# Output products ahead of the small convolution matmuls in pairs with in_proj alone, VectorE copies, later stores and later last scans

## The chip, the cores and the metric

The kernel runs on one core of a Trainium2 chip. The metric is the device time of one execution in microseconds (us), the median of several executions. A core has TensorE (PE) for matrix products, VectorE (DVE), ScalarE (ACT), GpSimd (POOL), and SyncE (SP), whose queue issues the DMA transfers here. TensorE writes its products to PSUM, 8 banks of 512 fp32 columns on 128 partitions. All data are fp32.

## The reference

For 4 images of 128 channels on 96x96 pixels, the reference normalises in groups of 4 channels (`_gn`), lays the pixels out in four orders (rows, rows reversed, columns, columns reversed), runs one sequence model on each, and fuses the four results.

```
def _scan1d(x, ...):
    t = _grouped1x1(x, in_proj_w, in_proj_b, G)
    u, gate = (t[:, :HID], t[:, HID:])
    u = jax.nn.silu(u)
    u = lax.conv_general_dilated(u, dw_w, ..., feature_group_count=HID)
    s = _conv1x1(u, ssm_in_w)
    a = DMIN + (DMAX - DMIN) * jax.nn.sigmoid(_conv1x1(u, ssm_delta_w, ssm_delta_b))
    a = jnp.clip(a, 0.0001, 0.9999)
    bb = jnp.tanh(_conv1x1(u, ssm_b_w, ssm_b_b))
    cc = jnp.tanh(_conv1x1(u, ssm_c_w, ssm_c_b))
    prefix = jnp.cumsum(jnp.log(a), axis=-1)
    hst = jnp.exp(prefix) * jnp.cumsum(bb * s * jnp.exp(-prefix), axis=-1)
    u = u + _conv1x1(cc * hst + ssm_d[None, :, None] * s, ssm_out_w)
    u = _grouped1x1(u * jax.nn.sigmoid(gate), mix_w, mix_b, G)
    return _conv1x1(u, out_proj_w, out_proj_b)
...
x = x + _L0_conv_ref(_gn(x), ...)
```

Here HID is 256 channels, the convolution has 5 taps, and the recurrent state has 32 channels. The log/exp/cumsum lines are the recurrence h = a*h + b*s.

## The kernel before, in words

**Tiling.** An image is done in two phases, one for the two column orders ("V") and one for the two row orders ("H"): 8 phases. In a phase two streams s = 0, 1 run together, which are one order and its reverse. A phase has 6 steps of 4 pairs. A pair (the function `pair(t)`, t from 0 to 191) takes one of 4 interleaved quarters of a step for both streams, 384 columns each. So a phase is 24 pairs, and t modulo 24 tells what a pair contains.

**Stages of a pair on TensorE**, with letters that the text uses:

- F, in_proj (`compute_front`), for the pair four ahead. The four results stand in banks 7, 6 (stream 0) and 2, 3 (stream 1), and ScalarE turns them into `sil` with a silu (L471). It is done only for the first 3 steps of a phase. The other 3 steps read the same columns backwards, with the streams exchanged. Steps 2 and 3 of a phase share a tile; the silus of steps 0 and 1 of a phase are stored to DRAM (L447, `kept_sil`) and loaded again.
- C, the convolution of the first 128 channels of u by `band` matrices (`conv`), and L, its remaining part with the small `less` matrices (`conv_less`), into one bank for each stream. ScalarE copies both banks to `us[i][:, s, 0, :]` (L589). The other 128 channels are convolved by VectorE, four `taps` at L606 after a first one on ScalarE (L604).
- W, the output product with `w_fin` (`accumulate`), for the pair seven back: a bank for each of two streams; ScalarE copies each to `ys` (L707, L709), and GpSimd adds it to `acc` in SBUF (L723).
- O, the state's product (`out_of`, L488), for the pair six back, into banks 0 to 3, which ScalarE has filled with u beforehand (`under`, L496) in many pairs. VectorE multiplies with the gates (`gating`, L558).
- G, the gates (`gate`, L482), in those pairs that make gates. ScalarE takes their tanh (L504).
- P, the projections (`proj`), always into banks 4 and 5. The first half of P reads the channels that VectorE convolved, the second those copied at L589. Then ScalarE (L634 to L636) and GpSimd make the recurrence's coefficients. VectorE runs the recurrence of a whole step in two scans (L676) in the first two pairs of the next step, and clips some coefficients (L764) in the last two. GpSimd makes the input of O from it (`outputs`, L682 to L684).

**Kinds of pairs**, by t modulo 24. 0 to 5 and 20 to 23: in_proj but no gates (the gates are old ones, loaded from DRAM); this is `with_front` and `old` in the code. 6 and 7: in_proj and gates. 8 to 17: gates alone. 18 and 19: neither. The first six pairs of the kernel have no `back` part (no W, O or gating). The last four pairs (188 to 191) have no in_proj.

**Banks.** `plan` gives C and W their banks. In a pair with in_proj, C and L use banks 4 and 5 and W uses 7 and 6. In the others it is the reverse.

**Order.** Each engine runs its instructions in the order in which the functions issue them; from `pair(0)` on the code is under a manual schedule. Before that (the first in_proj, statistics, weights) the framework orders them. In a pair with in_proj alone the TensorE order is F, C, L, W, O, P. In pairs with gates alone, and in those with neither, it is C, W, L, then G and O, or O alone, then P. The lines that decide it are L766 to L794 of `pair`. Between the stages of ScalarE in such a pair with in_proj alone stand, in this order: four silus, two copies of u, two `under`, two copies to `ys`.

After the 192 pairs, `tail()` finishes the last six units: it clips, runs the last step's two scans on VectorE, and then for each of six pairs O, gating, `under` of the next, W.

In the third and fourth pair of each step of a V phase of the first three images VectorE also takes statistics of the next image (`stats_chunks`, L397), and small pieces of `stats_finish` follow in the H phase.

Of the kernel before, what the change touches and what calls it, by code (L numbers as in the profile page):

```python
# [66 lines left out]
def conv_preact_kernel(  # L67
# [56 lines left out]
    def plan(with_front):  # L124

        return (PROJ, FRONT[:2]) if with_front else (FRONT[:2], PROJ)

    def bank(i):
        return psum[:, i, :]
# [119 lines left out]
    def load_front(step, s, r, q):  # L249
        if fresh(step):  # L250
            un = units[step * UB + s]
            nc.sync.dma_start(
                x_in[s][r, q, :], xs[un["b"], un["lay"], r, q, bass.ds(un["st"] * N, N + 1)]
            )
# [155 lines left out]
        for e in range(2)  # L410
    ]

    def front(i, banks, streams=range(2)):
        for _ in front_parts(i, banks, streams):
            pass

    def front_parts(i, banks, streams=range(2)):

        step, g = divmod(i, R)
        if step * UB >= NU:  # L420
            return
        st = step % NS
        if st == NS // 2:
            sils[step] = sils[step - 1]
            load_silu(step + 1, (g,))
        elif st == NS - 1 and g < 2:
            load_silu(step, (2 * g, 2 * g + 1))
        elif g == 0 and fresh(step):
            sils[step] = wk.tile([P, 2, 2, 4, N + 1], F32, tag="sil", name=f"sil_{step}")
        if fresh(step):  # L430
            yield from compute_front(step, g, banks, streams)
        sil = sils[step]

        if st == 0:
            engine = nc.gpsimd if step else nc.vector
            for s in range(2):
                engine.memset(sil[64 * s : 64 * s + 64, s, 0, g, 0:1], 0.0)
            if g < 2:
                engine.memset(sil[:, :, 1, g, 0:1], 0.0)

        for s in range(2):
            load_front(step + 1, s, slice(64 * s + 32, 64 * s + 64), slice(g, g + 1))
        if g == R - 1:
            for s in range(2):
                load_front(step + 1, s, slice(64 * s, 64 * s + 32), slice(0, R))
        if st < NS // 2 - 1:
            nc.sync.dma_start(kept_sil[step // NS % 2][st][g], sil[:, :, :, g, :])  # L447

    def load_silu(step, gs):
        if 0 in gs:  # L450
# [3 lines left out]
                sils[step][:, :, :, g, :], kept_sil[step // NS % 2][NS - 1 - step % NS][g]  # L454
            )

    def compute_front(step, g, banks, streams):
        un = units[step * UB]
        wn, bn = stats[un["b"]]
        sil = sils[step]  # L460
        for s in range(2):
            for j in range(2):
                r = slice(64 * s + 32 * j, 64 * s + 32 * j + 32)
                for c in range(4):
                    m, q = (c, g) if j else (g, R - 1 - c if s else c)
                    mm(bank(banks[2 * s + j]), c, wn[r, s, 32 * m : 32 * m + 32],
                       x_in[s][r, q, :], True, True)
        yield
        for s in streams:
            for j in range(2):  # L470
                nc.scalar.activation(  # L471
                    sil[:, s, j, g, :],
                    bank(banks[2 * s + j])[:, : N + 1],
                    AF.Silu,
                    bias=bn[:, 1:2] if j else bn[:, 4 + g : 5 + g],
                )
# [16 lines left out]
    def under(bi, s):  # L493

        seeded.add(bi)
        nc.scalar.copy(psum[:, SSM + 2 * s : SSM + 2 * s + 2, :N], us[bi][:, s])  # L496
# [80 lines left out]
                mm(bank(banks[s]), g, band[:, s, p, g, :], columns(step, sil[s][:, g, :], 1 - k),  # L577
                   True, False)

    def conv_less(i, banks):  # L580
        step, p = units[i]["step"], units[i]["p"]
        sil, k = blocks(step), less_of(p)
        for g in range(4):
            for s in range(2):
                r = less_rows(s, p)
                mm(bank(banks[s]), g, less[r, p, g, :], columns(step, sil[s][r, g, :], k),
                   False, True)
        for s in range(2):
            nc.scalar.copy(us[i][:, s, 0, :], bank(banks[s])[:, :N])  # L589

    def new_u(i):
        us[i] = wk.tile([P, 2, 2, N], F32, tag="u", bufs=LAG + 2, name=f"u_{units[i]['id']}")
# [149 lines left out]
    def pair(t):  # L742
        i, k, bi = 2 * t, t % R, 2 * (t - LAG)
        back = bi >= 0
        old = back and mirror(bi // 2) is not None

        late = bi > 2 and (bi - 2) % (NU // B) == 0
        with_front = fresh((t + R) // R)
        seed = old or back and not with_front
        banks, w = plan(with_front or not back)  # L750
        if back:
            front(t + R, FRONT, (1, 0) if old else (0, 1))
        if seed and not with_front:
            under(bi, 1)
        send()

        if len(reload) == 4 and (k == 1 or late):
            for b, r in reload:
                nc.sync.dma_start(accf[:, r], xr[b, :, r])
            reload.clear()  # L760
        new_u(i)
        taps(i, range(1, K))
        if t and clip_late(i - 2):
            nc.vector.tensor_scalar(*decay(i - 2)[1])  # L764
        conv(i, banks)
        if with_front or not back:  # L766
            conv_less(i, banks)
        if not back:
            first_tap(i + 2)
            front(t + R, FRONT)  # L770
        recurrence(t)
        un = units[i]
        stats_chunks(t)

        def stats_piece():
            if later and k > 1:
                next(later[0], None)

        if with_front or not back:
            free[0] = w[1]  # L780
            stats_piece()
        if seed and with_front:
            for s in (1, 0):
                under(bi, s)
        if waiting and not late:
            accumulate(waiting.pop(0), w[0])()
        if seed and not with_front:
            under(bi, 0)
        if old or not with_front:
            accumulate(waiting.pop(0), w[1])()  # L790
        if back and not with_front:
            free[0] = w[0]
            stats_piece()
            conv_less(i, banks)  # L794
        if old:
            for s in range(2):
                for j in range(2):
                    out_of(bi, s, j)
                load_gate(bi + s + UB)
        elif back:  # L800
            gates_and_out(bi, with_front)
        if back:
            for s in range(2):
                gating(bi, s)
        if un["order"] == "V" and un["b"] + 1 < B and un["st"] == NS - 1 and k == R - 1:
            later[:] = [stats_finish(un["b"] + 1)]
        if t + 1 < NU // 2:
            load_chunks(t + 1)
        if back:
            load_kept(bi // 2 + 2)  # L810
            if waiting:
                add = accumulate(waiting.pop(0), w[1])
                if not late:
                    add()
            first_tap(i + 2)
            scale_s(i - 2)
        if t == NU // 2 - 1:
            for s in range(2):
                under(bi + 2, s)
        proj(i, PROJ)  # L820
        if not back and t > 0:
            scale_s(i - 2)
        if late:
            add()
            accumulate(waiting.pop(0), w[1])()
        if back:
            waiting.extend(units[bi : bi + 2])
        if t == NU // 2 - 3:
            load_last()

        if bi > 0 and bi % (NU // B) == 0:
            send()

    def tail():

        first, banks = NU // 2 - LAG, (6, 7, 4, 5)

        for op in decay(NU - 2):
            nc.vector.tensor_scalar(*op)
        for part in range(2):  # L840
            scan(NU // UB - 1, part)
        scale_s(NU - 2)
        outputs(2 * first + 2)
        last = None
        for n in range(first, NU // 2):
            i = 2 * n
            for s in range(2):
                for j in range(2):
                    out_of(i, s, j)
            for s in range(2):  # L850
                gating(i, s)
                if i + 2 < NU:
                    under(i + 2, s)

            if last:
                last()
            if i + 4 < NU:
                outputs(i + 4, lambda *_: None)
            accumulate(waiting.pop(0), banks[2])()
            last = accumulate(waiting.pop(0), banks[3], nc.vector)  # L860
            if i + 4 < NU:
                nc.scalar.copy(tbs[i + 4][64:P, :], tbs[i + 4][0:64, :])
            send()
            waiting.extend(units[i : i + 2])
        last()
        for s in range(2):
            accumulate(waiting.pop(0), banks[2 + s], nc.vector, True)()
            send()
# [98 lines left out]
```

## Time and profile before

| what | us |
|---|---|
| five executions, median | 1872.89 |
| lowest and highest of them | 1872.38, 1874.05 |
| the profiled execution | 1873.79 |
| its span, first to last instruction | 1872.1 |
| ScalarE busy | 1544.7 |
| VectorE busy | 1553.5 |
| GpSimd busy | 1565.9 |
| pairs with in_proj alone, from one P to the next | 9.40 (the first of each four 9.46) |
| pairs with gates alone | 9.30 |
| pairs with neither | 8.25 |

The mean granted TensorE clock of the execution was 0.988. Read the span as stages, a pair of some 9 us each, since every stage has its own limit: the idle time of an engine in one pair says nothing of another. A timeline row names the start, the duration from the first start to the last end, the engine, the line, the operation, the tile written and those read, the shape, the number of instructions merged, and in brackets how long the engine had been idle before and what ended that. TensorE's rows overlap, since products are pipelined, so a stage's cost is the difference between its start and the next one's start. An fp32 product is two instructions in the counts.

### The profile page before, as it was taken

The numbers are of one execution on the slowest core, as the hardware profiler recorded it, in microseconds if no ns is written. First come the engines' busy times: TensorE is split into PE (matmuls) and PEld (weight loads), VectorE is DVE, ScalarE is ACT, GpSimd is POOL, SyncE is SP. The second block draws the span as 40 slices with busy tenths as digits, with TensorE's granted clock in tenths as the row PEclk, the third lists the DMA queues.
The fourth block names the chain that finished last, engine by engine and source line by source line (L and its number), as shares of the span: only waits on it lengthen the run. The fifth ranks groups of instructions, "written<-read, shape, count | busy, mean of one in ns | idle before, by whom it ended". The sixth has DMA issues, their size and how long they took to land. (4 is left out here: it accounts for less than half of the span.)

```text
span 1872.1 us, 57687 instructions
## 1 busy us (share of the span) xinstructions
PE 1833.6 (98%) x24024; PEld 691.7 (37%) x24024; DVE 1553.5 (83%) x1541; ACT 1544.7 (83%) x2873; POOL 1565.9 (84%) x1615
## 2 busy tenths in 40 slices
PE   5999999999999999999999999999999999999997
PEld 3234333443334433344333433344333443334432
DVE  4689888887888988888789898888887888788885
ACT  4788888888888888888888888888888888888875
POOL 5488988888879898888887989888888889988886
PEclk6999999999999999999999999999999999999998
DMA  7454473543875466243695556443476633635333
GB/s 241 118 192 155 140 220 100 174 151 127 274 249 189 155 183 208 84 158 121 207 298 190 170 167 202 143 139 117 156 232 217 231 136 125 205 100 171 145 130 142
DMA packets 147827, 321.20 MB, mean 172 GB/s; under 512 B 14192, under 2 KB 115696, under 8 KB 147568
## 3 DMA queue, kind: packets, MB, share of 16 engines
q1 hardware_dynamic: 147136, 316.56, 52.1%
q8 instruction: 190, 3.11, 0.7%
q10 hardware_dynamic: 432, 0.96, 0.1%
q14 instruction: 69, 0.57, 0.1%
HBM read 185.21 MB, written 132.25 MB: 170 GB/s over the span
## 5 line engine op out<-in xcount | busy, mean ns | idle before, releaser
L606 DVE SCALAR_TENSOR_TENSOR psum<-sil,small,psum 128x768 f32<-128x768 f32 x576 | 589.0, 1023 | 39.9 <-ACT psum L604 13.8
L133 PE MATMUL psum<-u,w_fin 128*32 128x384 f32 x6144 | 538.3, 489 | 0.3
L133 PE MATMUL psum<-u,main 128*32 128x384 f32 x6144 | 536.6, 490 | 0.7 <-DVE u L606 0.7
L558 DVE SCALAR_TENSOR_TENSOR u<-gate,psum 128x768 f32<-128x768 f32 x376 | 349.9, 953 | 199.4 <-ACT gate L504 86.8
L723 POOL TENSOR_TENSOR acc<-ys,acc 128x384 f32<-128x384 f32 x376 | 412.6, 1117 | 28.7 <-ACT ys L707 8.4
L682 POOL TENSOR_TENSOR t<-t,t 64x384 f32<-64x384 f32 x192 | 262.1, 1365 | 79.7 <-DVE t L676 66.5
L496 ACT COPY psum<-u 128x768 f32<-128x768 f32 x352 | 279.0, 810 | 40.2 <-DVE u L606 28.6
L133 PEld LDWEIGHTS psum<-u,w_fin 128*32 128x32 f32 x6144 | 189.0, 110 | 318.5 <-issue 219.4
L133 PEld LDWEIGHTS psum<-u,main 128*32 128x32 f32 x6144 | 182.3, 110 | 327.0 <-issue 247.3
L133 PE MATMUL psum<-sil,band 128*32 128x384 f32 x3072 | 289.0, 490 | 4.6 <-ACT tm L634 2.1
L683 POOL TENSOR_TENSOR t<-t,t 64x384 f32<-64x384 f32 x192 | 280.7, 1462 | 15.0
L639 POOL TENSOR_SCALAR t<-tm 64x384 f32<-64x384 f32 x191 | 177.6, 930 | 130.9 <-ACT tm L634 95.4
L604 ACT ACTIVATE psum<-sil,small 128x768 f32<-128x768 f32 x192 | 174.1, 907 | 125.9 <-DVE u L558 119.3
L488 PE MATMUL psum<-t,main 32*128 32x384 f32 x1536 | 239.4, 521 | 7.0 <-ACT psum L496 6.9
L642 POOL TENSOR_TENSOR t<-t,tm 64x384 f32<-64x384 f32 x192 | 208.9, 1088 | 15.3
L606 DVE SCALAR_TENSOR_TENSOR u<-sil,small,psum 128x768 f32<-128x768 f32 x192 | 194.9, 1015 | 7.8
L471 ACT ACTIVATE sil<-psum,bnorm 128x385 f32<-128x385 f32 x384 | 191.9, 584 | 10.8 <-PE psum L133 5.0
L504 ACT ACTIVATE gate<-psum,bnorm 128x384 f32<-128x384 f32 x384 | 193.4, 583 | 3.4 <-PE psum L488 1.8
L482 PE MATMUL psum<-x_in,wn 32*128 32x384 f32 x768 | 191.7, 521 | 0.4 <-ACT u L589 0.4
L709 ACT COPY ys<-psum 128x384 f32<-128x384 f32 x287 | 137.4, 479 | 53.3 <-PE psum L133 42.6
L589 ACT COPY u<-psum 128x384 f32<-128x384 f32 x384 | 165.4, 483 | 18.9 <-PE psum L133 13.1
L133 PE MATMUL psum<-sil,less 64*32 64x384 f32 x3072 | 168.4, 495 | 0.0
(86 smaller groups left out, 1637.1 us busy)
## 6 DMA issues: line engine op xcount, KB each, us to landing
sil<-sil SPq DMA_DIRECT2D x128, 770.0 KB, 6.2
kept<-gate SPq DMA_DIRECT2D x80, 768.0 KB, 3.9
gate<-kept SPq DMA_DIRECT2D x76, 768.0 KB, 4.9
x_in<-in_xs SPq DMA_DIRECT2D x192, 96.2 KB, 2.5
out<-acc SPq DMA_DIRECT2D x48, 384.0 KB, 6.1
acc<-in_xr SPq DMA_DIRECT2D x38, 384.0 KB, 6.3
xs<-in_xr SPq DMA_DIRECT2D x72, 192.0 KB, 5.2
x_in<-in_xs SPq DMA_DIRECT2D x184, 48.1 KB, 4.9
```

The costliest lines, as they stand in the source:

```text
L133: nc.tensor.matmul(o[r, : rhs.shape[-1]], lhsT, rhs, start=start, stop=stop, skip_group_check=True)
L471: nc.scalar.activation(sil[:, s, j, g, :], bank(banks[2 * s + j])[:, : N + 1], AF.Silu, bias=bn[:, 1:2] if j else bn[:, 4 + g : 5 + g],)
L482: nc.tensor.matmul(bank(to)[:, :N], stats[un["b"]][0][r, s, :], x_in[s][r, q, off : off + N], start=True, stop=True)
L488: nc.tensor.matmul(bank(SSM + 2 * s + j)[:, :N], w_so[r, bass.ts(j, P)], z[r, :], start=bi not in seeded, stop=True, skip_group_check=True)
L496: nc.scalar.copy(psum[:, SSM + 2 * s : SSM + 2 * s + 2, :N], us[bi][:, s])
L504: nc.scalar.activation(gv[:, s, j, :], bank(banks[2 * s + j])[:, :N], AF.Tanh, bias=bn[:, 2 + j : 3 + j], scale=0.5,)
L558: nc.vector.scalar_tensor_tensor(v, g, 1.0, pz, ALU.add, ALU.mult)
L606: nc.vector.scalar_tensor_tensor(us[i][:, :, 1, :] if k == K - 1 else part, src, w_tap[:, k : k + 1], part, ALU.mult, ALU.add,)
L642: nc.gpsimd.tensor_mul(ta[0:64, p, :], tb[0:64, :], tm[0:64, :])
L682: nc.gpsimd.tensor_mul(ta[0:64, p, :], tb[64:P, :], ta[64:P, p, :])
L683: nc.gpsimd.tensor_add(tb[0:64, :], ta[0:64, p, :], tb[0:64, :])
L723: adder.tensor_add(part, y, part)
```

## The change

Five edits, in `pair`, `front_parts`, `conv_less` and `tail`:

- In pairs with in_proj alone L comes after both W, as in the pairs without in_proj. ScalarE's copies of u follow the two copies to `ys` there. The piece of statistics moves with L.
- The silus of in_proj always begin with stream 0; they began with stream 1 in pairs with old gates.
- In pairs with gates alone that are third or fourth of their step (k > 1), VectorE copies u of stream 1 in place of ScalarE: t modulo 24 is 10, 11, 14 or 15, which is 32 pairs.
- The four stores of the first step's silu are issued at the end of pairs 0 to 3, where they were issued right after each silu, among the loads of the next step's in_proj columns.
- In the tail the last step's two scans follow the first pair's gating on VectorE.

```
-    def front_parts(i, banks, streams=range(2)):
+    def front_parts(i, banks):
...
+        if step:
+            keep_silu(step, g)
+
+    def keep_silu(step, g):
+        st = step % NS
         if st < NS // 2 - 1:
-            nc.sync.dma_start(kept_sil[step // NS % 2][st][g], sil[:, :, :, g, :])
+            nc.sync.dma_start(kept_sil[step // NS % 2][st][g], sils[step][:, :, :, g, :])
...
-        for s in streams:
+        for s in range(2):
...
-    def conv_less(i, banks):
+    def conv_less(i, banks, copies=(nc.scalar.copy, nc.scalar.copy)):
...
-        for s in range(2):
-            nc.scalar.copy(us[i][:, s, 0, :], bank(banks[s])[:, :N])
+        for s, copy in enumerate(copies):
+            copy(us[i][:, s, 0, :], bank(banks[s])[:, :N])
...
+        ahead = old or back and not with_front
         banks, w = plan(with_front or not back)
         if back:
-            front(t + R, FRONT, (1, 0) if old else (0, 1))
+            front(t + R, FRONT)
...
         conv(i, banks)
-        if with_front or not back:
+        if not ahead:
             conv_less(i, banks)
...
-        if with_front or not back:
+        if not ahead:
             free[0] = w[1]
             stats_piece()
...
-        if old or not with_front:
+        if ahead:
             accumulate(waiting.pop(0), w[1])()
-        if back and not with_front:
             free[0] = w[0]
             stats_piece()
-            conv_less(i, banks)
+
+            other = nc.vector.tensor_copy if k > 1 and not old else nc.scalar.copy
+            conv_less(i, banks, (nc.scalar.copy, other))
...
+        if t < R:
+            keep_silu(0, t)
...
         for op in decay(NU - 2):
             nc.vector.tensor_scalar(*op)
-        for part in range(2):
-            scan(NU // UB - 1, part)
         scale_s(NU - 2)
...
                 gating(i, s)
                 if i + 2 < NU:
                     under(i + 2, s)
+            if n == first:
+                for part in range(2):
+                    scan(NU // UB - 1, part)
```

More of the change, by code (lines that the diff above doesn't have):

```diff
@@ L411, in conv_preact_kernel, with front @@
     ]
-    def front(i, banks, streams=range(2)):
-        for _ in front_parts(i, banks, streams):
+    def front(i, banks):
+        for _ in front_parts(i, banks):
             pass
-    def front_parts(i, banks, streams=range(2)):
+    def front_parts(i, banks):
         step, g = divmod(i, R)
@@ L430, in front_parts @@
         if fresh(step):
-            yield from compute_front(step, g, banks, streams)
+            yield from compute_front(step, g, banks)
         sil = sils[step]
@@ L455, in load_silu, with compute_front @@
             )
-    def compute_front(step, g, banks, streams):
+    def compute_front(step, g, banks):
         un = units[step * UB]
```

## The prediction, made before the changed kernel was run

> **What bounds the kernel now.** I read the page's busy rows first, then TensorE's timeline stage by stage, then ScalarE's, then the two ends of the span.
>
> ```profile
> PE 1833.6 (98%) x24024; PEld 691.7 (37%) x24024; DVE 1553.5 (83%) x1541; ACT 1544.7 (83%) x2873; POOL 1565.9 (84%) x1615
> PEclk6999999999999999999999999999999999999998
> ```
>
> TensorE is busy for 98%, at full clock except in the first and last slice. Between the ends it is the bound, so a pair costs what TensorE needs for its stages. The next rows are pair 43 (19 modulo 24: neither gates nor in_proj, L already behind W), then pair 45 (21 modulo 24: in_proj alone, L ahead of W), each from the P before it to its own.
>
> ```profile
> 432.42 2.79 PE L133 MATMUL psum<-u,main 128*32 128x384 f32 x32
> 435.02 1.47 PE L133 MATMUL psum<-sil,band 128*32 128x384 f32 x16
> 436.31 2.76 PE L133 MATMUL psum<-u,w_fin 128*32 128x384 f32 x32
> 439.01 0.88 PE L133 MATMUL psum<-sil,less 64*32 64x384 f32 x16
> 439.81 0.93 PE L488 MATMUL psum<-t,main 32*128 32x384 f32 x8
> 440.67 2.79 PE L133 MATMUL psum<-u,main 128*32 128x384 f32 x32
> ...
> 450.13 2.79 PE L133 MATMUL psum<-u,main 128*32 128x384 f32 x32
> 452.85 0.94 PE L133 MATMUL psum<-x_in,wn 32*32 32x385 f32 x32
> 453.73 1.50 PE L133 MATMUL psum<-sil,band 128*32 128x384 f32 x16
> 455.15 0.88 PE L133 MATMUL psum<-sil,less 64*32 64x384 f32 x16
> 455.96 2.79 PE L133 MATMUL psum<-u,w_fin 128*32 128x384 f32 x32
> 458.68 0.93 PE L488 MATMUL psum<-t,main 32*128 32x384 f32 x8
> 459.53 0.85 PE L133 MATMUL psum<-u,main 128*32 128x384 f32 x8
> ```
>
> Start to start, pair 43 is P 2.60, C 1.29, W 2.70, L 0.80, O 0.86: 8.25 us. Pair 45 is P 2.72, F 0.88, C 1.42, L 0.81, W 2.72, O 0.85: 9.40. The same 16 C products take 0.13 more when L follows than when W follows. C and W have one tile shape (128*32), L another (64*32): each change of shape leaves a gap. Pair 45 has six changes; with L behind W it has five.
>
> **Edit 1, L behind both W (70 pairs).** t modulo 24 in 0 to 5 and 20 to 23 gives 10 pairs a phase. The first six pairs have no W and the last four no in_proj, so 7 x 10 = 70.
>
> Gain: C 1.42 to 1.29, W 2.72 to 2.70, which is 0.15. Cross-check: pair 43 plus F (0.88) plus P's longer end before F (0.12) is 9.25 against 9.40. 70 x 0.15 = 10.5 us.
>
> The Trainium skill, "TensorEngine Tiling (Array Packing)", Tiling Modes, Key Properties, says that a change of the mode, not of the tile, drains the engine. It gives no time. By the rule alone one could charge the 0.49 us that one product lasts (the page's row for w_fin): 70 x 0.49 = 34 us. The rows show 0.13 for that drain[...]. I take the rows.
>
> What may eat it is ScalarE, whose rows of the next pair (P at 459.53) follow.
>
> ```profile
> 463.62 2.00 ACT L471 ACTIVATE sil<-psum,bnorm 128x385 f32<-128x385 f32 x4
> 465.52 0.86 ACT L589 COPY u<-psum 128x384 f32<-128x384 f32 x2
> 466.27 1.55 ACT L496 COPY psum<-u 128x768 f32<-128x768 f32 x2
> 467.73 0.60 ACT L707 ACTIVATE ys<-psum,b_fin 128x384 f32<-128x384 f32 x1
> ```
>
> The copies of u now come last, and the next P may write bank 4 only after the first of them. Count from P: the silus begin at +4.09, end at +5.99; two `under` to +7.45 (VectorE's last tap ends at +6.32, in time); two `ys` to +8.4 (each W's products are done by +6.4 and +7.7). L starts at +7.57 and its products end 0.88 later, at +8.45; the copies start 0.09 after that (pair 45: L's end 456.03, copy 456.12). So bank 4 is free at +9.02, bank 5 at +9.40. P is due at +9.25 for bank 4 and 0.65 later for bank 5, and for the copied channels at +10.5. From a ScalarE end to the product that it releases, the trace has 0.14 (1841.08 to 1841.22) and 0.21 to 0.27 behind the copies of the gates-alone pairs. So P starts at +9.16 to +9.29: a stall of 0 to 0.04. I take 0. Both ends: 12 us gained if C and W also shed their rounding, 6 us if 0.06 stalls per pair remain. The silu order belongs to this: W needs bank 7 at +4.89, and with stream 0 first its silu is over at +4.67; with stream 1 first it would be over at +5.6 and the W would wait.
>
> VectorE (8.4 us a pair with scan, 1.3 idle before gating) and GpSimd stay below 9.25. The moved statistics piece puts one product behind the first `ys` in three pairs: at most 0.6 each, and it cost 0.6 to 0.9 there before. Nothing.
>
> **Edit 2, VectorE copies half of u (32 pairs).** In pair 36 (in this all gates-alone pairs run alike) the gate products of stream 1 follow the two copies in banks 7 and 6: the second copy ends at 376.08, its gate starts at 376.30, P at 376.98. The last O product starts at 376.28 and P never follows an O by less than 0.42, so P can come 0.28 earlier at most. VectorE starts when it is free. Its copy is not in the trace; nearest are its 128x384 adds at L723, 0.56 to 0.61, and ScalarE's own 0.48. I take 0.52. The skill ("Advanced Engine Details and Errata") has ScalarE nearer to PSUM and speaks against the move; by it VectorE would be the slower one, by its own adds it is about equal. What decides is what stands ahead in VectorE's queue: taps, clip, and in 12 of the 32 pairs two statistics (1.02 together). In pair 62 they end at 620.65, ScalarE's two copies at 620.52. There the copy ends at 621.17, 0.65 late, and P with it. Listing all 32 pairs by VectorE's free time: 17 gain 0.1 to 0.28 (together 4.0 us), 15 lose 0.04 to 0.66 (together 5.6, less about 0.7 where two follow each other). Sum +1; ends -5 (copy at 0.4, clips shorter) and +5.
>
> **Edit 3, four stores later.**
>
> ```profile
> 38.56 1.13 PE L133 MATMUL psum<-sil,less 64*32 64x384 f32 x16
> 43.73 2.20 PE L133 MATMUL psum<-x_in,wn 32*32 32x385 f32 x32 [4.03 <-DMA x_in<-in_xs]
> ```
>
> The SP queue issues three stores of 770 KB among the loads; the last x_in loads are issued at 35.50 and reach TensorE at 43.73. Without the stores the last product that they overwrite is over at 33.2, four issues take 3.0, and an undisturbed load lands in 2.6 to 3.1: 39. L ends at 39.4. So F comes 4.3 earlier. P then took 4.5 instead of 2.7 at half clock, which followed the idle stretch: up to 1.8 more. But the stores join pairs 0 to 3, where the loads for the statistics already hold VectorE (1.2 to 3.1 us of DMA wait at 60 and 70) and P waits for VectorE from pair 3 on. I give back 1.6: -4.5; ends -7 and 0.
>
> **Edit 4, last scans later.**
>
> ```profile
> 1832.12 2.79 PE L133 MATMUL psum<-u,w_fin 128*32 128x384 f32 x32
> 1841.22 2.42 PE L488 MATMUL psum<-t,main 32*128 32x384 f32 x8 [6.31 <-ACT psum L496]
> 1843.57 5.07 PE L133 MATMUL psum<-u,w_fin 128*32 128x384 f32 x32
> ```
>
> Gating waits for two scans (2.54, 2.55), `under` for gating, O for `under`. Then W takes 5.0 instead of 2.7. Now gating ends at 1835.9, O runs at about 1837 to 1838.5 (GpSimd's copy), W to 1841.7. What is late next is ScalarE: its copy of the third pair's state waits for scans (1841.0) and two GpSimd operations (2.4), and `under` stands behind it at about 1844.0, as before. So the third O starts at about 1845 instead of 1848.57, the second W at 1846.7 instead of 1849.43: -2.7. It rests on the clock. The skill ("TensorE: Matmul & The Clock Gate", Part 1) halves it after an idle window of about 3.4 us; the granted clock here is 0.50 in 1841 to 1845 after 6.3 idle. The new gaps are some 2 and 3.2 us. By the rule, unhalved: -2.7; halved again: 0. I take -2.5, ends -5 and +1.
>
> **Sum.** -10.5 + 1 - 4.5 - 2.5 = -16.5. The profiled execution took 1873.79 (span 1872.1 and 1.7 around it), so 1857.3; that execution is 0.9 above the median shown, so 1856.4.
>
> **Rivals.**
> - **Copies hold P (gain given back).** Were the first copy 0.15 later than counted (a slower release, PSUM shared with VectorE), edit 1 gives nothing: -6 remain, 1867. For it: the margin is 0.1 to 0.2. Against: bank 5 and the second half of P have 0.5 and more.
> - **Slower: the same queue, further.** If `ys` and `under` run late, so that bank 4 comes free beyond +9.5, the pair is 9.7: 70 x 0.3 = 21, less 6, 1888. It turns slower than before when P stalls by over 0.15 + 6/70 = 0.24. For it: four more ScalarE instructions stand ahead of the copies. Against: ScalarE's rows above leave them done at +8.4.
> - **The edits at the ends do nothing** (DMA as loaded, clock halved again): edits 1 and 2 alone, -9.5, 1863.
> - **Edit 2 loses in all pairs** (copy 0.7): 32 x 0.35 = +11 in place of +1, 1867.
>
> **Chances.** Forecast 0.62, first rival 0.12, slower rival 0.07, ends 0.12, edit 2 0.07. The forecast's own bounds are 1847 and 1864; taking in the rivals near 1867 gives 1846 to 1868. What measurement can tell is 0.2%, 3.7 us. Faster 0.86, same 0.05, slower 0.09.
>
> **What would show it.** In pairs with in_proj alone: C 1.29 and a pair of 9.25, with P's row free of a ScalarE wait. In the 32 pairs: P earlier by 0.28 in those without statistics, later in the V phases. F at about 39.4 in place of 43.73. O of the second tail pair near 1837 less the shift, W at 2.7. It is wrong if pairs with in_proj alone stay at 9.40 with P waiting for the copy of u, or if VectorE's copy takes over 0.6.

## The result, and the profile after

The changed kernel takes 1869.98 us (median of 31 executions, 1866.47 to 1874.45), the kernel before 1873.37 (52 executions, 1869.6 to 1878.51). The ratio is 0.9982, with a 95% interval of 0.9977 to 0.9987: 3.4 us faster, where 16.5 were forecast. The profiled execution took 1867.5 us with a span of 1865.8. That is 6.3 less than the span of before, but this execution is among the quicker of its 31 (third), so its profile shows more gain than the medians do.

The page of after, its busy row and the granted clock by slice:

```profile
PE 1825.3 (98%) x24024; PEld 691.4 (37%) x24024; DVE 1561.8 (84%) x1573; ACT 1542.5 (83%) x2841; POOL 1566.6 (84%) x1615
PEclk7999999999999999999999999999999999999999
```

TensorE is still the bound. VectorE took over 32 copies (1541 to 1573 instructions), ScalarE lost them. The last digit of the clock rose from 8 to 9: the halved clock of the tail is gone. To see where the 6.3 us came from, I took the start of each pair's P in both traces and summed by kind of pair:

| stretch of the span | before, us | after, us | change |
|---|---|---|---|
| start to the P of pair 0 | 45.85 | 40.39 | -5.5 |
| P of pair 0 to P of pair 6 | 45.43 | 52.40 | +7.0 |
| 70 pairs with in_proj alone | 664.03 | 657.25 | -6.8 |
| 32 pairs in which VectorE copies | | | +1.7 |
| the other pairs from pair 7 on | | | +1.1 |
| P of pair 191 to the end | 43.69 | 39.88 | -3.8 |

Two terms stand out against the forecast. What the stores gave at the start is lost, and more, before pair 6. And the 70 pairs give 6.8 of 10.5 here, though most of the single pairs do what was forecast. TensorE's rows of after, pair 49 (1 modulo 24, in_proj alone), from P to P:

```profile
488.25 2.79 PE L133 MATMUL psum<-u,main 128*32 128x384 f32 x32
490.96 0.95 PE L133 MATMUL psum<-x_in,wn 32*32 32x385 f32 x32
491.84 1.50 PE L133 MATMUL psum<-sil,band 128*32 128x384 f32 x16
493.15 2.77 PE L133 MATMUL psum<-u,w_fin 128*32 128x384 f32 x32
495.85 0.88 PE L133 MATMUL psum<-sil,less 64*32 64x384 f32 x16
496.65 0.93 PE L493 MATMUL psum<-t,main 32*128 32x384 f32 x8
497.51 2.79 PE L133 MATMUL psum<-u,main 128*32 128x384 f32 x32
```

C to W is 1.31 (before 1.42 to L), W 2.70, and the pair 9.26. P has no bracket: it does not wait.

Now the opening. C of pair 5 before, and then TensorE's rows of after, F and P of pair 0 and pairs 3 to 5:

```profile
78.64 1.79 PE L133 MATMUL psum<-sil,band 128*32 128x384 f32 x16 [0.45 <-ACT tm L634]
```

```profile
39.43 1.03 PE L133 MATMUL psum<-x_in,wn 32*32 32x385 f32 x32
40.39 2.79 PE L133 MATMUL psum<-u,main 128*32 128x384 f32 x32
...
68.32 1.39 PE L133 MATMUL psum<-x_in,wn 32*32 32x385 f32 x32 [0.69 <-DMA x_in<-in_xs]
69.64 2.79 PE L133 MATMUL psum<-u,main 128*32 128x384 f32 x32
78.50 2.79 PE L133 MATMUL psum<-sil,band 128*32 128x384 f32 x16 [6.07 <-ACT tm L639]
```

ScalarE in the same stretch, and the SP queue, which issues the DMAs (the duration of an SP row is the issuing, not the transfer):

```profile
69.11 0.91 ACT L609 ACTIVATE psum<-sil,small 128x768 f32<-128x768 f32 x1 [0.52 <-DVE u L611]
75.98 2.00 ACT L476 ACTIVATE sil<-psum,bnorm 128x385 f32<-128x385 f32 x4 [5.96 <-DMA xs<-in_xr]
```

```profile
60.95 2.88 SPq L252 DMA_DIRECT2D x_in<-in_xs  x4
64.54 1.47 SPq L452 DMA_DIRECT2D sil<-sil  x2
66.11 2.56 SPq L393 DMA_DIRECT2D xs<-in_xr  x2
```

The row at 64.54 holds two stores, the last of the second step's silu and, at 65.16, the last of the first step's. That one, with its time from issue to landing at the end:

```profile
sil<-sil SPq DMA_DIRECT2D x1, 770.0 KB, 10.6
```

At 69.64 the P of pair 4 runs. Then ScalarE stands for 5.96 us before the four silus of pair 4, the coefficients behind them (L639) are late, and TensorE stands for 6.07 us before C. C then takes 2.79 in place of 1.8, since the granted clock is halved from 76.3 to 83.1. Pair 5 takes 14.08 us (before 6.71). The bracket names the load of `xs`, which a silu doesn't read. The silus of pair 4 write the tile of the phase's third step. The code takes these tiles from a pool of two, so it is the first step's tile used again, and it may be written only when the first step's stores have read it. The times agree with that: the fourth store landed at 75.80 (65.16 and 10.6), and the silu began 0.18 later, at 75.98. The two loads of `xs` issued behind it landed at about 76.3 and 76.8, when the silu was already running, so they can't have held it. The kernels with edit 3 alone, without edit 3 and without these stores (`e3_late_stores`, `e5_no_late_stores`, `e10_no_first_stores`) test this reading.

### The profile page after: what moved, and what is told of

Read it like the earlier page. It is cut to its first block, busy times and chain, and to the rows that moved or that the text cites. A ratio compares the mean times of both kernels' runs of the same rounds, so it can differ in the third digit from the quotient of the medians.

```text
span 1865.8 us, 57669 instructions
## 1 busy us (share of the span) xinstructions
PE 1825.3 (98%) x24024; PEld 691.4 (37%) x24024; DVE 1561.8 (84%) x1573; ACT 1542.5 (83%) x2841; POOL 1566.6 (84%) x1615
## 4 chain that ended last, share of the span: by engine, by line
PE 86%; ACT 4%; DVE 3%; POOL 2%; DMA 2%; issue 1%; SPq 0%; POOLq 0%; ACTq 0%; DVEq 0%
PE psum L133 72%; PE psum L493 7%; PE psum L487 7%; ACT sil L476 1%; DVE psum L611 1%; ACT psum L609 1%; DVE u L563 1%; DMA xs<-in_xr 1%; POOL acc L728 1%; DMA sil<-sil 1%; ACT u L594 1%; POOL t L644 0%; DMA x_in<-in_xs 0%; ACT tm L639 0%; POOL t L687 0%
## 5 line engine op out<-in xcount | busy, mean ns | idle before, releaser
L133 PEld LDWEIGHTS psum<-u,w_fin 128*32 128x32 f32 x6144 | 195.4, 110 | 301.1 <-issue 221.0
L594 ACT COPY u<-psum 128x384 f32<-128x384 f32 x352 | 153.1, 482 | 30.7 <-PE psum L133 22.5
L714 ACT COPY ys<-psum 128x384 f32<-128x384 f32 x287 | 132.5, 475 | 47.6 <-PE psum L133 39.7
```

What stands on the lines that cost most here:

```text
L133: nc.tensor.matmul(o[r, : rhs.shape[-1]], lhsT, rhs, start=start, stop=stop, skip_group_check=True)
```

## The experiments

Two theories stood at the beginning. By the first, edit 3 moves a wait from the first loads to the reuse of the store's buffer, and this takes what edits 1 and 4 give. Its rival was that L behind W costs its gain back in the pairs with in_proj alone, as the copies of u hold P. Each edit was therefore made alone first. Every time below stands against executions of the kernel before that were measured beside it, so the figure for before differs from group to group. The ratio and its interval come from all executions of both and need not be the quotient of the two medians.

**Edit 1 alone** (`e1_less_behind_w`, repeated later as `e11_less_again`).

```
+        ahead = old or back and not with_front
...
-            front(t + R, FRONT, (1, 0) if old else (0, 1))
+            front(t + R, FRONT)
...
-        if with_front or not back:
+        if not ahead:
             conv_less(i, banks)
...
-        if old or not with_front:
+        if ahead:
             accumulate(waiting.pop(0), w[1])()
-        if back and not with_front:
             free[0] = w[0]
```

> The kernel before with edit 1 alone (L behind both W and the silu order). Theory A (TensorE saves one change of tile shape, 0.14 us in each of 70 pairs): about 10 us faster, 0.995. Theory B (GpSimd's queue is too full at the start of phases 1, 3, 5 and 7, and the scan that waits for it gives some back, as in the changed kernel, where 70 pairs sum to -6.8): 6 to 8 us faster, 0.996, with pairs of 10.2 to 10.4 us at 0 or 1 modulo 24. Rival (copies of u hold P): nothing.

Measured: 1869.11 us against 1871.99, ratio 0.9981 (0.9970 to 0.9991).

> Edit 1 alone once more. The first run's profiled execution was the fastest of its twelve. Theory (TensorE's saving of 0.14 in 70 pairs is there in every execution; the rest of the spread are waits for transfers in single pairs): the 70 pairs again at 9.26 or 9.33 but for some, median 3 to 6 us under before. Rival (the saving exists only in fast executions): the usual pair is 9.40 again.

Measured: 1869.97 against 1873.54, ratio 0.9979 (0.9970 to 0.9987). Edit 1 is worth 2.9 and 3.6 us in the medians, less than either theory said. Its pairs take 9.26 and P waits for no copy: "copies hold P" is refuted. The silu order was changed with it and wasn't tried alone. The 70 pairs together took 656.0 and 658.8 us in the two profiled executions, where 70 x 0.14 off the 664.0 of before would give 654.2.

**Edit 2 alone** (`e2_vector_copy`).

```
-            conv_less(i, banks)
+            other = nc.vector.tensor_copy if k > 1 and not old else nc.scalar.copy
+            conv_less(i, banks, (nc.scalar.copy, other))
```

> The kernel before with edit 2 alone (VectorE copies u of stream 1 in 32 pairs). Theory: 1.7 us slower as in the changed kernel's 32 pairs, 1.001, with pairs of V phases at 14 modulo 24 near 10.0 and those without statistics near 9.05. Rival (the copies cost nothing and the trace differs by chance): no change.

Measured: 1875.0 against 1871.99, ratio 1.0017 (1.0008 to 1.0026). The 32 pairs cost 1.65 us more in its trace, and 1.71 in the changed kernel's. Pair 62 is one with statistics. ScalarE's two copies in it before, and then VectorE's rows of the changed kernel:

```profile
619.66 0.86 ACT L589 COPY u<-psum 128x384 f32<-128x384 f32 x2
```

```profile
618.25 1.35 DVE L771 TENSOR_SCALAR t<-t 64x384 f32<-64x384 f32 x1
619.63 1.02 DVE L397 BATCH_NORM_STATS2 bn<-xs 128x6 f32<-128x384 f32 x2
620.56 0.54 DVE L594 COPY u<-psum 128x384 f32<-128x384 f32 x1
621.40 0.95 DVE L563 SCALAR_TENSOR_TENSOR u<-gate,psum 128x768 f32<-128x768 f32 x1 [0.30 <-ACT gate L509]
```

The copy takes 0.54. It stands behind clip and statistics and ends at 621.10, which is 9.1 us after the P of pair 61 (611.98). ScalarE's two copies of before were over at 620.52, 8.4 after that P (612.10). Pair 62 is 0.7 longer. Of the 32 pairs, 13 gain 0.09 to 0.26 us in the changed kernel's trace (2.7 together), 11 lose 0.19 to 0.74 (4.5 together), and 8 stay within 0.03.

**Edit 3 alone** (`e3_late_stores`), the four stores at the end of pairs 0 to 3.

```
+        if t < R:
+            keep_silu(0, t)
```

> The kernel before with edit 3 alone (the first step's four silu stores at the end of pairs 0 to 3). Theory (the silus of step 2 are written into the buffer that the stores still read; ScalarE waits about 6 us in pair 5, and TensorE's clock halves there): the first P 5 us earlier and pair 6's P 1.5 us later than before, so 1 to 3 us slower, 1.001. Rival (the loss in pair 5 comes from another edit): 5 to 7 us faster, 0.997.

Measured: 1875.77 against 1871.99, ratio 1.0015 (1.0006 to 1.0024). The P of pair 0 is at 40.62 (before 45.85), but that of pair 6 at 93.45 (before 91.28): 5.2 earlier has become 2.2 later. The silu of pair 4 stands for 5.30 us here. The fourth store, issued at 65.15, took 11.3 and landed at about 76.5, and the silu began at 76.66. Alone, with no other edit, it makes the kernel slower.

**Edit 4 alone** (`e4_late_scans`), the two scans behind the first gating of the tail.

```
-        for part in range(2):
-            scan(NU // UB - 1, part)
...
+            if n == first:
+                for part in range(2):
+                    scan(NU // UB - 1, part)
```

> The kernel before with edit 4 alone (last scans behind the first gating). Theory (no idle window before the second W, so that the clock stays whole): 3.8 us faster, 0.998, as between the last pair's P and the end of the two traces. Rival (in many executions the gap of 3 us still halves the clock): 0 to 2 us faster.

Measured: 1870.05 against 1871.99, ratio 0.9985 (0.9976 to 0.9994). The tail, from the P of pair 191 to the end, takes 39.85 us. In the five traces that have this edit it is 39.85 to 40.06. In the nine without it, before twice among them, it is 42.2 to 43.7, mean 42.9: 3.0 us gained, 0.8 less than the two traces compared at first had shown.

**All but edit 3** (`e5_no_late_stores`), the changed kernel with the first stores where they were.

> The changed kernel with edit 3 taken back (stores where they were). Theory (edit 3 costs 1 to 4 us net, by the wait of the silus of pair 4 for the fourth store): faster than the changed kernel by that much, 0.996 to 0.997 of before, and no wait of ScalarE in pair 5. Rival (the cost of the late stores was noise): as the changed kernel, 0.998.

Measured: 1867.93 against 1873.81, ratio 0.9964 (0.9951 to 0.9977). The changed kernel's ratio is 0.9982, so edit 3 costs it about 0.0018, some 3 us. The two intervals only touch, at 0.9977. In its trace the P of pair 6 is at 90.27 (92.79 in the changed kernel), and pair 5 takes 6.70.

**The stores earlier** (`e6_stores_in_pairs_0_1`), before with two of them at the end of pair 0 and two at the end of pair 1. If only the landing of the last two counts, this frees the buffer in time.

```
+        if t < 2:
+            keep_silu(0, 2 * t)
+            keep_silu(0, 2 * t + 1)
```

> The kernel before with edit 3 in another form: two of the four stores at the end of pair 0 and two at the end of pair 1. Theory (the loss is the wait for the fourth store, which was issued at 66 us and landed near 76): the stores land by about 62, pair 5 takes about 7 us again, and P of pair 6 comes 3 to 6 us earlier than before, 0.997 to 0.998. Rival (the loss is DMA load as such, wherever the stores stand): 0 to 2 us slower, as with edit 3.

Measured: 1878.35 against 1873.81, ratio 1.0020 (1.0009 to 1.0030). I expected better. Its TensorE rows:

```profile
60.58 1.01 PE L133 MATMUL psum<-x_in,wn 32*32 32x385 f32 x32
66.36 4.94 PE L133 MATMUL psum<-u,main 128*32 128x384 f32 x32 [4.77 <-DVE u L611]
...
77.50 4.48 PE L133 MATMUL psum<-u,main 128*32 128x384 f32 x32 [2.41 <-DVE u L611]
```

The 6-us wait before C that edit 3 brought is gone, but P now waits 4.77 and 2.41 for VectorE in pairs 3 and 4, and the first of them runs at half clock (0.52 granted in 66 to 71). VectorE stood for its statistics, and those for the loads of `xs`:

```profile
60.07 0.56 DVE L397 BATCH_NORM_STATS2 bn<-xs 128x6 f32<-128x384 f32 x1 [6.38 <-DMA xs<-in_xr]
...
71.54 0.56 DVE L397 BATCH_NORM_STATS2 bn<-xs 128x6 f32<-128x384 f32 x1 [4.74 <-DMA xs<-in_xr]
```

So the P of pair 6 is at 94.85, 3.6 later than before. Issued late the stores hold the buffer; issued early they stand ahead of the loads for the statistics, and those come late.

**The stores left out** (`e10_no_first_stores`), to price them. The kernel has no call of `keep_silu` for the first step. The last step of the first phase loads the second step's silus instead.

```
+        if step:
+            keep_silu(step, g)
...
-                sils[step][:, :, :, g, :], kept_sil[step // NS % 2][NS - 1 - step % NS][g]
+                sils[step][:, :, :, g, :], kept_sil[step // NS % 2][1 if step == NS - 1 else NS - 1 - step % NS][g]
```

> The kernel before without the four stores of the first step's silu; the last step of the first phase loads the second step's in their place, so part of that phase is computed from other data. Theory (the stores cost the start 5 us where they were, and where edit 3 puts them they cost it again through the wait of pair 4's silu): P of pair 0 about 5 us earlier, and P of pair 6 still about 6.5 earlier, 0.9965. Rival (pairs 1 to 5 are held by other transfers anyhow): P of pair 6 less than 3 us earlier.

Measured: 1868.19 against 1873.54, ratio 0.9970 (0.9959 to 0.9980). Its TensorE rows of pairs 4 and 5, and the silus on ScalarE that stood for 5.96 us in the changed kernel:

```profile
68.54 2.79 PE L133 MATMUL psum<-u,main 128*32 128x384 f32 x32
71.87 1.78 PE L133 MATMUL psum<-sil,band 128*32 128x384 f32 x16 [0.54 <-ACT tm L639]
...
75.33 2.79 PE L133 MATMUL psum<-u,main 128*32 128x384 f32 x32
```

```profile
69.35 2.00 ACT L476 ACTIVATE sil<-psum,bnorm 128x385 f32<-128x385 f32 x4
```

The P of pair 0 is at 40.15, as with edit 3, and the wait in pair 5 is gone: 6.79 us in place of 14.08. The P of pair 6 is at 84.50, 6.8 earlier than before (91.28; 89.7 to 91.4 in the nine traces that have the stores where they were). The loads of `xs`, which the bracket had named, are still issued here, so it was the stores. All that could be had from the first stores is thus about 7 us of span (5.4 in the medians), and neither of the two moves tried gets any of it.

**The parts that pay, with early stores** (`e7_kept_parts`): edits 1 and 4, edit 2 only in the 16 of its pairs that have no statistics ahead of the copy and are not 35 modulo 48 (a pair that had lost 0.4 in the trace), and the stores as in `e6_stores_in_pairs_0_1`.

```
-            other = nc.vector.tensor_copy if k > 1 and not old else nc.scalar.copy
+            other = nc.vector.tensor_copy if k > 1 and not old and not chunks_of(t) and t % (2 * NP) != 35 else nc.scalar.copy
```

> Edits 1 and 4, edit 2 only in pairs without statistics of the next image on VectorE, edit 3 with the stores in pairs 0 and 1. If the parts add up as measured one by one (-3 to -8, -2 to -4, about -3, -3 to -6): 0.990 to 0.994 of before. Rival (GpSimd takes over as the bound at the start of the phases): 0.995.

Measured: 1870.7 against 1873.81, ratio 0.9981 (0.9971 to 0.9991). The selected copies now gain 0.98 us over the 32 pairs (in place of a loss of 1.7). But the early stores lose as before, and the 70 pairs took 660.9. One of them shows a second way in which the gain of edit 1 can be lost. TensorE's rows at pair 72, the first of a phase:

```profile
702.83 2.79 PE L133 MATMUL psum<-u,main 128*32 128x384 f32 x32
705.98 0.88 PE L133 MATMUL psum<-x_in,wn 32*32 32x385 f32 x16 [0.36 <-DMA x_in<-in_xs]
707.80 0.94 PE L133 MATMUL psum<-x_in,wn 32*32 32x385 f32 x16 [0.94 <-DMA x_in<-in_xs]
708.67 2.79 PE L133 MATMUL psum<-sil,band 128*32 128x384 f32 x16
711.23 3.09 PE L133 MATMUL psum<-u,w_fin 128*32 128x384 f32 x32
```

F finds its input columns not yet loaded, twice, and C and part of W run slow after it: 13.09 us for this pair, 3.8 more than the 9.33 of the same pair in `e1_less_behind_w`. Divided by 0.14, that is the gain of 27 pairs.

**GpSimd relieved** (`e8_less_and_clip`). In the traces with edit 1, pairs 25, 73, 121 and 169 (the second pair of every other phase) often took 10.1 to 10.5 instead of 9.26. The changed kernel shows why at pairs 24 and 25, first GpSimd, then VectorE, then F of pair 25 on TensorE:

```profile
256.77 0.94 POOL L644 TENSOR_SCALAR t<-tm 64x384 f32<-64x384 f32 x1
257.79 0.94 POOL L644 TENSOR_SCALAR t<-t 64x384 f32<-64x384 f32 x1
258.81 1.02 POOL L647 TENSOR_TENSOR t<-t,tm 64x384 f32<-64x384 f32 x1
```

```profile
259.86 2.86 DVE L681 TENSOR_TENSOR_SCAN t<-t,t 64x768 f32<-64x768 f32 x1 [1.62 <-POOL t L647]
```

```profile
263.97 1.53 PE L133 MATMUL psum<-x_in,wn 32*32 32x385 f32 x32
```

The same scan before:

```profile
257.44 2.88 DVE L676 TENSOR_TENSOR_SCAN t<-t,t 64x768 f32<-64x768 f32 x1 [0.62 <-POOL t L642]
```

The scan waits 1.62 us for GpSimd's product, where it waited 0.62. Gating of pair 24 stands behind it on VectorE, and F of pair 25, half of which goes into banks that this gating reads, takes 1.53 us where it usually takes 0.95. GpSimd has no gap there. So the experiment has edit 1, and gives the second clip of each phase's last pair to VectorE.

```
-        return units[i]["p"] in (1, 2)
+        return units[i]["p"] in (1, 2) or i // 2 % NP == NP - 1
```

> Edit 1 alone, and the last pair of each phase leaves its second clip to VectorE in the next pair, which takes 0.9 us from GpSimd ahead of the first scan of a phase. Theory (GpSimd's backlog there eats what edit 1 saves): the pairs of 9.9 to 10.4 us at 0 and 1 modulo 24 go down by 0.5 or more, 2 to 4 us faster than edit 1 alone, 0.996. Rival (the scan waits for something else): as edit 1 alone, 0.998.

Measured: 1870.07 against 1873.81, ratio 0.9980 (0.9969 to 0.9991). The same place in its trace, GpSimd and VectorE:

```profile
254.89 0.96 POOL L639 TENSOR_SCALAR t<-tm 64x384 f32<-64x384 f32 x1
255.92 1.02 POOL L642 TENSOR_TENSOR t<-t,tm 64x384 f32<-64x384 f32 x1
```

```profile
257.49 2.55 DVE L676 TENSOR_TENSOR_SCAN t<-t,t 64x768 f32<-64x768 f32 x1
```

The scan has no bracket any more, and the four pairs take 9.31, 9.61, 9.26 and 9.26, together 2.4 and 1.7 us less than in the two traces with edit 1 alone. So that mechanism is shown at its place. Yet the median is that of edit 1 alone. A gain of 2 us is about what the interval leaves open, and in this trace other places are late, as in other traces with edit 1: pair 120 took 10.71 and pair 104, where GpSimd adds to a reloaded `acc`, 12.53 (10.74 before).

**The kernel before once more** (`e12_before_again`), to see how far single pairs repeat.

> The kernel before, unchanged, to see what differs between two executions of one program. Theory: the pairs repeat to 0.02 us but for single ones at 0 and 8 modulo 24, in the first six pairs and in the tail, which differ by 1 to 2 us as transfers and the clock fall. Rival: all pairs shift a little.

Measured: 1870.53 in one execution, span 1868.8 (1872.1 in the first profile). The 70 pairs sum to 662.7 against 664.0, nearly all of the difference in pair 24 (9.47 against 10.92). In all seven traces without edit 1 this sum is 662.5 to 664.0. In the seven with it, it is 655.8 to 660.9. So edit 1 gains 1.6 to 8.2 us in these pairs, depending on which two traces are compared, and 4.6 between the means (663.1 and 658.5). The other pairs from 7 on, without the 32 of edit 2, take 1.3 more with it (means 774.2 and 775.5), which leaves about 3, as in the medians. Its pairs are surely shorter, and the traces with it have more long pairs: in pairs 24, 72, 104 and 120 those above 10 us (for pair 104, whose usual time is 10.75, above 11) number fourteen in the seven traces with edit 1, and three in the seven without. Counted from the shortest time that each pair took in the seven traces with edit 1, the pairs 25, 73, 121 and 169 cost edit 1 about 2.6 us (mean of the six traces without the moved clip), and pairs 24, 72 and 120 cost 0.7 to 4.4, mean 2.9 (in the seven without it, counted in the same way, 0 to 1.5, mean 0.3).

**Without edit 3, copies chosen** (`e9_best_without_3`): edits 1 and 4, and the copies selected as in `e7_kept_parts`.

> Edits 1 and 4, and edit 2 only in pairs where VectorE has no statistics ahead of the copy; edit 3 left out. Theory (the parts add, each measured alone): edit 1 -7, edit 4 -3, edit 2 -1, so 10 to 12 us less in the trace and, with waits for transfers that differ from run to run, 0.994 to 0.996. Rival (waits for transfers take what is saved): 0.998.

Measured: 1863.76 (1862.09 to 1866.04, 6 executions) against 1873.54, ratio 0.9949 (0.9937 to 0.9961). It beats both kernels: 9.8 us under before, and its interval lies below the changed kernel's.

## Why the prediction was wrong

The direction was right, the size was not: 16.5 us forecast, 3.4 measured in the medians and 6.3 in the profiled executions.

Of the 10.2 us by which the profiled execution fell short, edit 3 makes 6.0, edit 1 makes 3.7, edit 2 and the other pairs 1.8, and the tail gave 1.3 more than forecast.

- **Edit 3, "-4.5; ends -7 and 0": the first step that failed.** F did come at 39.43 where 39.4 was forecast, and P ran unhalved. The failed sentence is "I give back 1.6". It priced the stores only as load on the DMA beside the statistics, and never asked who next writes the tile that they read. That is the silu of pair 4, on ScalarE, ahead of the coefficients for which TensorE waits. The wait that was put at nothing measured 5.96 us of ScalarE and 6.07 of TensorE. The measured effect is +1.5 to +2.2 us at pair 6 and about +3 in the times (`e3_late_stores`, `e5_no_late_stores`), outside both ends. The price of the stores themselves (6.8 us, `e10_no_first_stores`) fits the "-7", which neither move tried reached.
- **Edit 1, "70 x 0.15 = 10.5": the second step that failed.** The pair is right (9.40 to 9.26, 0.14 against 0.15), and so is the count for bank 4: P doesn't wait. The failed sentence is that VectorE "and GpSimd stay below 9.25". It compared averages over a pair, and it left the loads out. In the pairs at a phase's start GpSimd has no gap, and there the scan's wait grew from 0.62 to 1.62 us. The 70 pairs gave 1.6 to 8.2 us from trace to trace, 4.6 between the means, and the whole about 3 in the medians. The place in pairs 25, 73, 121 and 169 is shown by `e8_less_and_clip`. That late transfers in pairs 24, 72, 104 and 120 are more frequent with edit 1 is seen in the counts above; that they are so because TensorE comes earlier to loads that are only just in time is my guess and not shown.
- **Edit 2, "+1"**: +1.7 in the trace and +3.0 in the medians, within its ends, the copy 0.54 against 0.52 taken. So "loses in all pairs (copy 0.7)" is refuted. Seventeen pairs were to gain 4.0 us, and 13 gained 2.7. What decides is what stands ahead of the copy, as forecast: leaving out the pairs with statistics and 35 modulo 48 turned the loss into a gain of 1.0.
- **Edit 4, "-2.5"**: 3.0 over many traces, 1.9 in the medians. TensorE's rows of the changed kernel's tail:

```profile
1829.65 2.79 PE L133 MATMUL psum<-u,w_fin 128*32 128x384 f32 x32
1833.91 0.91 PE L493 MATMUL psum<-t,main 32*128 32x384 f32 x2 [1.48 <-POOL t L688]
1835.83 0.92 PE L493 MATMUL psum<-t,main 32*128 32x384 f32 x6 [1.01 <-POOL t L689]
1836.68 2.79 PE L133 MATMUL psum<-u,w_fin 128*32 128x384 f32 x32
1841.34 1.56 PE L493 MATMUL psum<-t,main 32*128 32x384 f32 x8 [1.87 <-POOL acc L728]
1842.83 2.79 PE L133 MATMUL psum<-u,w_fin 128*32 128x384 f32 x32
```

The gaps of 1.0 to 1.9 us leave the clock whole (granted 1.00 from 1829 to 1847), and each W takes 2.7 where the second took 5.0. Counted from the P of pair 191, the rest of the second O comes at +9.9 (1835.83 less 1825.90), where 1837 to 1838.5 was +8.6 to +10.1: it waits for GpSimd's copy (L689), as forecast. The third O comes at +15.4; the forecast's 1845 was +16.6, before had +20.2. The chain is the one forecast: ScalarE's copy of the third pair's state (1839.99) stood 4.72 us for GpSimd's two operations, which had waited for the scans, and `under` followed at 1840.40. Of these 4.8 us the later rounds give about 1 back: from O to O they take 4.2 and 3.8 where before took 3.6.

- **The rivals.** The two at 1867 came nearest in time, by mechanisms that aren't there: the copies don't hold P, and VectorE's copy doesn't take 0.7. "The edits at the ends do nothing" is right for the sum of the ends, about 3 us lost at one and 3 gained at the other, but not for its reasons, and its 1863 takes edits 1 and 2 as forecast. "Slower: the same queue, further" is refuted by P, which doesn't wait. That the single parts sum to so little is seen in their ratios: 0.9981, 1.0017, 1.0015 and 0.9985 make 0.9998, and the whole is 0.9982, each with some 0.001 of interval.

What stays open is why the loads of `x_in` at 24, 72 and 120 and the reload of `acc` at 104 are late in some executions and not in others, and whether a third buffer for the silus would free the first stores; it wasn't tried. The kernel that did best, `e9_best_without_3`, gained more than its parts alone (the ratios 0.9981 and 0.9985 and 1.0 us of copies make 0.996), but with 6 executions that is within the intervals.

## What to carry to other kernels

When a store is moved later, look for the next writer of the buffer that it reads, and count from issue to landing, not only the load on the queue. A saving per stage is multiplied only as long as every other engine and each transfer has slack in that very pair, so check the stages with the least slack and not the mean. When one edit of several fails, make the others alone: here edits 1 and 4 with the good half of edit 2 made 0.9949, where all together made 0.9982.

## What was not expected of the hardware

- Four stores of 770 KB cost 6.8, 9.0 and 10.4 us by the P of pair 6 (91.28, 93.45 and 94.85 against 84.50 without them) at the three places tried in the first 70 us. These are single traces: over all of them the P of pair 6 is at 89.7 to 91.4, 92.8 to 93.5 and 94.0 to 94.9. The eight stores that the changed kernel issued from 43 to 66 us took 5.6 to 10.6 us from issue to landing (median 8.0).
- Two executions of one kernel agree to some 0.02 us in most pairs (180 of 191 in the kernel before, 174 with edit 1 alone), and differ by 1 to 2 us in a few (pair 24: 9.47 and 10.92 in the kernel before; pair 72: 9.33 and 11.49 with edit 1 alone). Among kernels with edit 1 pair 24 reached 13.19 (`e5_no_late_stores`).
- In pair 72 of `e7_kept_parts` TensorE waited only 0.36 and 0.94 us, yet C behind it took 2.56 in place of 1.3, start to start, at a granted clock of 0.58 (708 to 711). Gaps of 1.48, 1.01 and 1.87 us in the tail of the changed kernel left the clock at 1.00. The length of the idle stretch alone doesn't tell these two apart, and no run here says what does.
